# A selective scan on one core: pairs of channel blocks taken in turn, and the sums over states run in quarters of the array

## The chip, the cores and the metric

The kernel runs on one core of one Trainium2 chip. The metric is device time in microseconds (us) of one launch. Before the change three runs took 21455.4, 21479.64 and 21486.99 us; their median is 21479.64 us. One further execution was recorded by the hardware profiler; all views shown here are of that one.

## The reference, cut to what matters

Four layers follow each other on eight images of 56 x 56 tokens with 192 channels: a Toeplitz gate, windowed attention, a depthwise convolution, and a state space layer (a selective scan in four directions). The change lies in the last. Its core, per image, direction and channel (384 channels, 16 states, 3136 tokens):

```python
delta = jax.nn.softplus(delta + delta_bias[None, :, :, None])
dA = jnp.exp(delta[:, :, :, None, :] * A[None, :, :, :, None])
dBu = (delta * u)[:, :, :, None, :] * Bm[:, :, None, :, :]
# hs[t] = dA[t] * hs[t - 1] + dBu[t], for each channel and state
y = jnp.einsum('bkdnl,bknl->bkdl', hs, Cm)     # the sum over the 16 states
return y + Dp[None, :, :, None] * u
```

The four directions' y are added; a normalization over the 384 channels with gain `ln_g` and bias `ln_b`, a product with silu(z) and a projection `out_proj_w` to 192 channels follow, and the result is added to the layer's input.

## The kernel before, in words

All data are fp32. A tensor is laid out with channels on the 128 partitions, so the 384 channels are three blocks d = 0, 1, 2, and tokens lie along the free dimension. The tokens of an image are cut into seven chunks of 448. Directions are called slots; they run in the order 2, 3, 0, 1.

**Stages.** Up to about 3423 us the kernel makes the convolution kernels of the Toeplitz layer, that layer's products for all images, and the whole preparation (`front`, L944: `gate`, `attention`, `conv2`, `inner`, `steps`) of image 0. From there to the end the scan runs: 8 images x 4 directions x 7 chunks = 224 chunks. The front of image b + 1 runs beside the scan of image b, and `finish` (L951) runs for each chunk of the last direction, beside the scan as well.

**The scan.** A chunk holds 24 pairs, numbered g over the whole scan (list `pairs`, L1018): three channel blocks d, and for each of them k = 0..7, where a pair stands for two states (NG = 2). In the order before, all eight k of one d follow each other. For one pair:

- `inject` (L1059, GpSimd): du times B into a slot of `ring` (six slots).
- `decay` (L1076, ScalarE): two exponentials into a bank pair `ps_a` of PSUM (two of them).
- `scan` (L1085, VectorE): the recurrence. It writes over the ring slot if `on_pool(d, k)` holds and over the PSUM tile otherwise.
- `times_c` (L1091): times C into `hc`, of which there are four buffers. It runs on GpSimd where `on_pool` holds (even k) and on VectorE otherwise.
- `keep_state` (L1098) and `initial` (L1066), ScalarE: two columns each.
- `add_up` (L1106, TensorE): for each of the two states a matmul of `ident` (128 x 128) with `hc`, which adds hc to a bank `ps_y` in PSUM. There are two such banks; one holds the sum of one block d over all 16 states.
- `sums` (L1116 in slot 2, else L1118, VectorE): adds the bank to `ysum` in SBUF once all eight k are in; in slot 2 it also adds D times x, for which the x tile is loaded again (`load_xc`, L1032).

An fp32 matmul appears in the trace as two MATMUL records, each with its LDWEIGHTS record, so L1106 has four of each per pair.

**What sets the order.** Scheduling is written out by hand. The loop over g (from L1259) emits for each step: the injection for g + 2 (`feed`), the GpSimd product of pair g - 1, the decay of g + 1, the scan of g, the VectorE product of g if it is one, perhaps a `sums`, then `parts.step`, which emits pieces of `front` and `finish` where a planner (`Parts`, L1121) with rough costs per engine thinks that they fit, and last `add_up(g - 2)`. Each engine's queue is in order, so whatever `parts.step` put on TensorE stands ahead of that `add_up`. The planner emits at most one bank of a client's matmuls in a step: a generator yields `(held, needs)` and stops while it holds a bank. The two banks `ps_f` are for these pieces. The planner counts `add_up` as 1.1 us of TensorE per pair, through `summed[g - 2] = run("E", 1.1, ...)`.

`sums(i, d - 1)` is emitted at k = 4 of the next block, three steps after the last `add_up` of its bank; its x tile is asked for at k = 2. B and C for the next chunk are loaded (`load_bc`, L1027) one k at a time during d = 2. DMAs of the scan and of the front share the SP queue; `inner` stores silu(z) with one DMA per block at L888.

## Time and profile before

| what | value |
|---|---|
| median of three runs | 21479.64 us |
| the profiled execution's own time | 21510.71 us |
| its span, first to last instruction | 21508.5 us |
| first and last scan instruction | 3423 and 21472 us |
| TensorE busy | 17461.0 us (81%) |
| VectorE busy | 15779.7 us (73%) |
| GpSimd busy | 15095.0 us (70%) |
| ScalarE busy | 12490.5 us (58%) |
| mean granted TensorE clock | 0.865 |

How to read it: busy shares are means over stages with different limits, so the stretches of one image's scan have to be taken apart. Names in the profile: PE is TensorE, PEld its weight loads, DVE is VectorE, ACT is ScalarE, POOL is GpSimd, SP is the queue that issues most DMAs. A busy PE is not a PE at its peak, since the end of a matmul includes time in which the next one already runs; the distance between two starts tells how many fit. A group's line shows "busy us, mean ns of one | idle of its engine just before it, and what ended that idle time".

### The profile page before, as it was taken

To read this page: it belongs to the slowest core of one execution; us is meant where nothing else is said; L and a number is where in the kernel's file an instruction comes from. 1 tells how busy PE (TensorE), PEld (TensorE's weight loads), DVE (VectorE), ACT (ScalarE), POOL (GpSimd) and SP (SyncE) were. 2 spreads that over 40 slices of the span, in tenths; PEclk is the share of its full clock that TensorE was granted. 3 is DMA by queue.
4 is the path that set the end of the run, shared out by engine and by line. 5 is a ranking of instruction groups with operands and counts; after the bars stand their busy time and mean duration, and the time that the engine had idled before them with its cause. 6 is when DMAs were issued, how large, how long until landed. Compare 5 with 4: busy or idle time off the path is not lost. (4 is left out here: it accounts for less than half of the span.)

```text
span 21508.5 us, 203992 instructions
## 1 busy us (share of the span) xinstructions
PE 17461.0 (81%) x59404; PEld 9086.2 (42%) x59404; DVE 15779.7 (73%) x12469; ACT 12490.5 (58%) x31833; POOL 15095.0 (70%) x9176
## 2 busy tenths in 40 slices
PE   7878678887887789877987788879877888787777
PEld 4845455433443344433543354334433443333333
DVE  2122116996799668977898779867987789789998
ACT  3126113666666566757575657666666667575555
POOL 0000005887788678867897778878887788689999
PEclk9587757998998889888998899889988999888888
DMA  3931676456544755466545654565446554754444
GB/s 88 248 97 39 190 211 181 131 159 213 172 142 134 217 166 152 134 183 199 160 128 172 209 157 138 159 212 170 140 148 214 173 146 132 218 180 147 134 131 128
DMA packets 2566532, 3470.45 MB, mean 161 GB/s; under 512 B 936270, under 2 KB 2518704, under 8 KB 2534578
## 3 DMA queue, kind: packets, MB, share of 16 engines
q1 hardware_dynamic: 2542724, 3340.61, 52.4%
q0 software_dynamic: 15520, 116.14, 1.5%
q8 instruction: 473, 7.75, 0.2%
q14 instruction: 647, 5.30, 0.1%
q10 hardware_dynamic: 7168, 0.65, 0.0%
HBM read 2822.68 MB, written 634.11 MB: 161 GB/s over the span
## 5 line engine op out<-in xcount | busy, mean ns | idle before, releaser
L1106 PE MATMUL ps_y<-hc,ident_sb 128*128 128x448 f32 x21504 | 10003.9, 603 | 828.4 <-POOL hc L1091 750.6
L1059 POOL TENSOR_TENSOR ring<-du,bm 128x896 f32<-128x896 f32 x5376 | 9450.8, 1775 | 745.8 <-ACT ring L1066 383.2
L1076 ACT ACTIVATE ps_a<-delta,A_logs_sb 128x449 f32<-128x449 f32 x10752 | 6859.6, 638 | 354.3 <-DVE ring L1085 97.7
L1106 PEld LDWEIGHTS ps_y<-hc,ident_sb 128*128 128x128 f32 x21504 | 4315.8, 210 | 5154.2 <-issue 3636.4
L1091 POOL TENSOR_TENSOR hc<-ring,cm 128x896 f32<-128x896 f32 x2688 | 4769.2, 1774 | 1930.7 <-DVE ring L1085 922.1
L1085 DVE TENSOR_TENSOR_SCAN ps_a<-ps_a,ring 128x898 f32<-128x898 f32 x2688 | 5428.3, 2019 | 607.8 <-ACT ps_a L1076 558.2
L1085 DVE TENSOR_TENSOR_SCAN ring<-ps_a,ring 128x898 f32<-128x898 f32 x2688 | 5424.1, 2018 | 571.8 <-ACT ps_a L1076 407.1
L1091 DVE TENSOR_TENSOR hc<-ps_a,cm 128x896 f32<-128x896 f32 x2688 | 2935.2, 1092 | 1037.6 <-PE ps_y L1106 808.0
L1098 ACT COPY state<-ps_a 128x2 f32<-128x2 f32 x2687 | 426.5, 159 | 2783.3 <-DVE hc L1091 2775.4
L287 DVE COPY tzx<-ps_tz 112x448 f32<-112x448 f32 x432 | 269.9, 625 | 1442.5 <-PE ps_tz L281 1292.4
L281 PE MATMUL ps_tz<-tzx,tm 112*112 112x112 f32 x4608 | 1031.1, 406 | 344.7 <-DMA tm<-ext 295.9
L295 POOL DMA_DIRECT2D o<-tzx x192 | 97.3, 513 | 1579.6 <-DVE tzx L287 1341.0
L281 PEld LDWEIGHTS ps_tz<-tzx,tm 112*112 112x112 f32 x4608 | 1021.8, 319 | 385.7 <-issue 381.9
L1066 ACT COPY ring<-state 128x2 f32<-128x2 f32 x4608 | 823.0, 179 | 532.2 <-POOL hc L1091 531.1
L666 PE MATMUL ps_f<-ident_sb,slab 98*98 98x98 f32 x1344 | 336.5, 325 | 602.9 <-ACT slab L659 602.7
L1098 ACT COPY state<-ring 128x2 f32<-128x2 f32 x2688 | 504.1, 188 | 489.6 <-DVE ring L1085 476.2
L1042 POOL TENSOR_TENSOR du<-delta,xcd 128x448 f32<-128x448 f32 x672 | 659.8, 982 | 20.0 <-DMA slab<-in_w_p_dram 19.6
L83 PE MATMUL ps_f<-slab 96*32 96x448 f32 (+7 forms) x2432 | 588.4, 548 | 75.9 <-DMA slab<-pad 55.9
L234 PE MATMUL ps_qv<-wqv,xn 96*128 96x384 f32 (+1 forms) x1200 | 530.3, 525 | 135.6 <-ACT sl L236 68.0
L666 PEld LDWEIGHTS ps_f<-ident_sb,slab 98*98 98x98 f32 x1344 | 202.5, 157 | 1017.5 <-ACT slab L659 798.5
L503 PE MATMUL ps_f<-ident_sb,slab 112*96 112x112 f32 x4704 | 534.7, 268 | 99.7 <-DVE slab L511 49.8
L503 PEld LDWEIGHTS ps_f<-ident_sb,slab 112*96 112x96 f32 x4704 | 513.1, 170 | 239.0 <-issue 121.6
(221 smaller groups left out, 16398.9 us busy)
## 6 DMA issues: line engine op xcount, KB each, us to landing
bm<-bc SPq DMA_DIRECT2D x1792, 448.0 KB
cm<-bc SPq DMA_DIRECT2D x1792, 448.0 KB
xcd<-xc SPq DMA_DIRECT2D x840, 224.0 KB
dl<-slab SPq DMA_DIRECT2D x224, 672.0 KB
delta<-dl SPq DMA_DIRECT2D x224, 672.0 KB
slab<-pad SPq DMA_DIRECT2D x504, 232.0 KB
tzx<-qv SPq DMA_DIRECT2D x192, 588.0 KB
o<-tzx POOLq DMA_DIRECT2D x192, 588.0 KB, 14.2
```

Of the source, the lines that this page charges most:

```text
L83: return f(*args, **kw)
L281: nc.tensor.matmul(po[:, c, :], t[:, :, c2 + c], x[:, :, c1 + c2 + c], start=True, stop=True)
L503: nc.tensor.matmul(p[:CP, t * TT : (t + 1) * TT], ot[:, n % 2, i, t, c % 2 * CP : c % 2 * CP + CP], ident[:TT, :TT], start=i == 0, stop=i ...
L666: nc.tensor.transpose(p[:PT_, e * PT_ : (e + 1) * PT_], S[:, 3 * g + e, :], ident[:PT_, :PT_])
L1042: nc.gpsimd.tensor_mul(du[:, 0, :], deltas[i][:, d, 1 : CH + 1], xcs.pop((i, d)))
L1059: nc.gpsimd.tensor_mul(hs[:, :, tokens(i)[0]], dus[i, d].to_broadcast([128, NG, CH]), bms[i, k])
L1066: nc.scalar.copy(in_ring(g)[:, :, tokens(i)[1]], src)
L1076: nc.scalar.activation(dA[:, n, :], deltas[i][:, d, at : at + CH + 1], AF.Exp, scale=negA[:, slot, d, c : c + 1])
L1085: nc.vector.tensor_tensor_scan(h, dA, hs, 0.0, ALU.mult, ALU.add)
L1091: (nc.gpsimd if on_pool(d, k) else nc.vector).tensor_mul(hc, h[:, :, tokens(i)[0]], cms[i, k])
L1098: nc.scalar.copy(states[i][:, d, NG * k : NG * k + NG], h[:, :, tokens(i)[2]])
L1106: nc.tensor.matmul(yps[i, d][:, :CH], ident, hcs[g][:, n, :], start=k + n == 0, stop=k + n == NP + NG - 2)
```

## The change

1. **Order of pairs.** For each chunk the blocks d = 0 and d = 1 take turns: (0, k = 0), (1, k = 0), (0, k = 1), and so on for 16 steps; d = 2 follows with its eight. `on_pool` becomes "d = 0, or d = 2 and k even", so even steps of a chunk still multiply by C on GpSimd and odd ones on VectorE.
2. **`add_up` runs every second step, for two pairs.** For d = 2 it makes the same four matmul calls for two pairs as before. For a pair of d = 0 and d = 1 with the same k it makes, for each state n, four calls of 64 x 64: `ident[rows, rows]` with half the partitions of one hc. Rows 0-63 of both blocks go to bank u = 0 (block 0's to partitions 0-63, block 1's to 64-127), rows 64-127 of both to bank u = 1 (block 0's to 64-127, block 1's to 0-63). So two banks are open at once, and each holds halves of both blocks.
3. **What follows from mixed banks.** `ysum[:, 0]` and `ysum[:, 1]` hold mixed channels; D, `ln_g`, `ln_b` and `w_out` are permuted on the host (`mixed`), silu(z) is stored mixed (two DMAs of 64 partitions in place of one for d < 2), and the x tile of slot 2 is loaded by `load_mixed` (two DMAs in place of one).
4. **When things are emitted.** With `at` the step in the chunk: `sums` for banks 0 and 1 at 17 and 18, for bank 2 at step 1 of the next chunk; the x tiles of slot 2 at 12, 15 and 21; a wait for `ending` at 16 in place of 12. Other loads stay at their steps.
5. **The planner's books.** `run("E", ...)` is called once per two pairs: 1.1 for d < 2, 2.2 for d = 2.

The core of the diff:

```diff
-        pairs = [(i, d, k) for i in range(len(chunks)) for d in range(ND) for k in range(NP)]
+        pairs = [
+            (i, d, k) for i in range(len(chunks)) for ds in ((0, 1), (2,)) for k in range(NP) for d in ds
+        ]
...
-            return k % 2 == 0
+            return d == 0 or d == 2 and k % 2 == 0
...
             if k == 0:
-                yps[i, d] = psy.tile([128, 512], F32, name="ps_y")
+                for u in (0, 1) if d == 0 else (2,):
+                    yps[i, u] = psy.tile([128, 512], F32, name="ps_y")
+            if d == 2:
+                for q in range(2):
+                    for n in range(NG):
+                        nc.tensor.matmul(
+                            yps[i, 2][:, :CH],
+                            ident,
+                            hcs[g + q][:, n, :],
+                            start=k + q + n == 0,
+                            stop=k + q + n == NP + NG - 2,
+                        )
+                return
+            lo, hi = slice(0, 64), slice(64, 128)
             for n in range(NG):
-                nc.tensor.matmul(
-                    yps[i, d][:, :CH], ident, hcs[g][:, n, :], start=k + n == 0, stop=k + n == NP + NG - 2
-                )
+                for u, at, q, rows in ((0, lo, 0, lo), (0, hi, 1, lo), (1, hi, 0, hi), (1, lo, 1, hi)):
+                    nc.tensor.matmul(
+                        yps[i, u][at, :CH],
+                        ident[rows, rows],
+                        hcs[g + q][rows, n, :],
+                        start=k + n == 0,
+                        stop=k + n == NP + NG - 2,
+                    )
...
-                done = (i, d - 1) if d else (i - 1, ND - 1)
-                if k == 2 and g > NP and chunks[done[0]][1] == 2:
-                    xds[done] = load_xc(*done)
+                if slot == 2 and at in (12, 15, 21):
+                    u = (12, 15, 21).index(at)
+                    xds[i, u] = load_mixed(i, u)
...
-                if k == 4 and g > NP:
-                    sums(*done)
+                if at in (17, 18):
+                    sums(i, at - 17)
+                if i and at == 1:
+                    sums(i - 1, 2)
...
-                if g >= 2:
+                if g and g % 2 == 0:
                     add_up(g - 2)
-                    summed[g - 2] = run("E", 1.1, taken[g - 2])
+                    summed[g - 2] = summed[g - 1] = run("E", 1.1 if d < 2 else 2.2, taken[g - 2], taken[g - 1])
```

and in `inner`, and the new loader:

```diff
-                    nc.sync.dma_start(out=dst[:, d, :], in_=src)
+                    if dst is z_d[b] and d < 2:
+                        for h in range(2):
+                            to = (h ^ d) * 64
+                            nc.sync.dma_start(out=dst[to : to + 64, h, :], in_=src[64 * h : 64 * h + 64])
+                    else:
+                        nc.sync.dma_start(out=dst[:, d, :], in_=src)
...
+        def load_mixed(i, u):
+            b, slot, j = chunks[i]
+            t = sp.tile([128, CH], F32, name="xcd", bufs=3)
+            for h in range(2):
+                half, d = (slice(64 * u, 64 * u + 64), u ^ h) if u < 2 else (slice(64 * h, 64 * h + 64), 2)
+                src = xc_d[slot // 2][b][half, d, j * CH : (j + 1) * CH]
+                nc.sync.dma_start(out=t[64 * h : 64 * h + 64], in_=src)
+            return t
```

More of the change, by code (lines that the diff above doesn't have):

```diff
@@ L1103, in add_up, with sums @@
             if k == 0:
-                yps[i, d] = psy.tile([128, 512], F32, name="ps_y")
-            for n in range(NG):
-                nc.tensor.matmul(
-                    yps[i, d][:, :CH], ident, hcs[g][:, n, :], start=k + n == 0, stop=k + n == NP + NG - 2
-                )
-        def sums(i, d):
+                for u in (0, 1) if d == 0 else (2,):
[12 more added lines that the diff above has]
+            lo, hi = slice(0, 64), slice(64, 128)
+            for n in range(NG):
+                for u, at, q, rows in ((0, lo, 0, lo), (0, hi, 1, lo), (1, hi, 0, hi), (1, lo, 1, hi)):
[6 more added lines that the diff above has]
+                    )
+        def sums(i, u):
             b, slot, j = chunks[i]
-            y = yps[i, d][:, :CH].rearrange("p (u v) -> p u v", v=H)
-            yv = scan_view(ysum[:, d], slot, j)
+            y = yps[i, u][:, :CH].rearrange("p (u v) -> p u v", v=H)
+            yv = scan_view(ysum[:, u], slot, j)
             if slot == 2:
-                x = xds.pop((i, d)).rearrange("p (u v) -> p u v", v=H)
-                nc.vector.scalar_tensor_tensor(yv, x, Dsum[:, d : d + 1], y, ALU.mult, ALU.add)
+                x = xds.pop((i, u)).rearrange("p (u v) -> p u v", v=H)
+                nc.vector.scalar_tensor_tensor(yv, x, Dsum[:, u : u + 1], y, ALU.mult, ALU.add)
             else:
@@ L1261, in model @@
                     b_next += 1
-                more = i + 1 < len(chunks)
-                if more and d == 1 and k == 0:
+                more, at = i + 1 < len(chunks), g % (ND * NP)
+                if more and at == 8:
                     b1, slot1, j1 = chunks[i + 1]
@@ L1269, in model @@
                         xcs[i + 1, e] = load_xc(i + 1, e)
-                if more and (d, k) == (2, 0):
+                if more and at == 16:
                     xcs[i + 1, 2] = load_xc(i + 1, 2)
-                if more and (d, k) in ((1, 6), (1, 7), (2, 6)):
-                    times_x(i + 1, k - 6 if d == 1 else 2)
+                if more and at in (14, 15, 22):
+                    times_x(i + 1, min(at - 14, 2))
                     run("P", 0.93)
@@ L1293, in model @@
                     load_bc(pi + 1, pk)
-                done = (i, d - 1) if d else (i - 1, ND - 1)
-                if k == 2 and g > NP and chunks[done[0]][1] == 2:
-                    xds[done] = load_xc(*done)
-                if i % (4 * NCH) == 0 and b > 0 and (d, k) == (1, 4):
+                if slot == 2 and at in (12, 15, 21):
+                    u = (12, 15, 21).index(at)
+                    xds[i, u] = load_mixed(i, u)
+                if i % (4 * NCH) == 0 and b > 0 and at == 16:
                     while ending.at < 3:
                         parts.step(anything, ending)
-                if k == 4 and g > NP:
-                    sums(*done)
+                if at in (17, 18):
+                    sums(i, at - 17)
+                if i and at == 1:
+                    sums(i - 1, 2)
                 pb, pslot, pj = chunks[i - 1]
-                if i and pslot == 1 and (d, k) == (0, 5):
+                if i and pslot == 1 and at == 5:
                     while ending in parts.clients:
@@ L1310, in model @@
                 parts.step({"A": max(n2, fed[g + 2]) - 0.7, "E": n1 + 5.0, "D": 0.2})
-                if g >= 2:
+                if g and g % 2 == 0:
                     add_up(g - 2)
-                    summed[g - 2] = run("E", 1.1, taken[g - 2])
-            if on_pool(d, k):
-                times_c(last)
-            for g in (last - 1, last):
-                add_up(g)
+                    summed[g - 2] = summed[g - 1] = run("E", 1.1 if d < 2 else 2.2, taken[g - 2], taken[g - 1])
+            add_up(last - 1)
             while parts.clients:
                 parts.step(anything)
-            sums(i, d)
+            sums(i, 2)
             drain(finish(b, j))
@@ L1356, in parts, with mixed @@
         return v.reshape((-1, p) + v.shape[1:]).swapaxes(0, 1)
+    def mixed(v):
+        w = v.copy()
+        w[64:, 0], w[:64, 1], w[64:, 1] = v[:64, 1], v[64:, 1], v[64:, 0]
+        return w
     def with_bias(w, b):
@@ L1401, in layouts @@
     a["A_logs"] = np.asarray(i[p + "A_logs"]).reshape(4, ND, 128, NS)[order].transpose(2, 0, 1, 3)
-    a["Ds"] = np.asarray(i[p + "Ds"]).reshape(4, ND, 128).transpose(2, 1, 0)
-    a["ln_g"], a["ln_b"] = parts(i[p + "ln_g"], 128), parts(i[p + "ln_b"], 128)
-    a["w_out"] = parts(np.asarray(i[p + "out_proj_w"]).T, 128)
+    a["Ds"] = mixed(np.asarray(i[p + "Ds"]).reshape(4, ND, 128).transpose(2, 1, 0))
+    a["ln_g"], a["ln_b"] = mixed(parts(i[p + "ln_g"], 128)), mixed(parts(i[p + "ln_b"], 128))
+    a["w_out"] = mixed(parts(np.asarray(i[p + "out_proj_w"]).T, 128))
     a.update(constants())
```

## The prediction

> **What bounds the kernel now.** I read the page first, then the stretches of one image's scan, then the waits, and last the order of time inside two stretches. From the page, the busy row of TensorE and the groups that the change touches or that stand behind it (busy us, mean ns, idle time before it and what ended it):

> ```profile
> PE 17461.0 (81%) x59404; PEld 9086.2 (42%) x59404; DVE 15779.7 (73%) x12469; ACT 12490.5 (58%) x31833; POOL 15095.0 (70%) x9176
> L1106 PE MATMUL ps_y<-hc,ident_sb 128*128 128x448 f32 x21504 | 10003.9, 603 | 828.4 <-POOL hc L1091 750.6
> L1091 DVE TENSOR_TENSOR hc<-ps_a,cm 128x896 f32<-128x896 f32 x2688 | 2935.2, 1092 | 1037.6 <-PE ps_y L1106 808.0
> ```

> The adds over states are the largest TensorE group, and VectorE's products stand still 808 us for them: an hc buffer is free only after its add. The mean hides the stages, so here are the scan of image 3 cut by direction (beside it run gate and attention; attention; conv2 and inner; steps, finish and the next gate), and 14 chunks of the last image, beside which no front runs. Columns: length, then PE, PEld, DVE, ACT, POOL busy, clock, DMA.

> ```profile
> 10430.00:10973.00 543.00, 476.47 (x1764) 253.78 (x1763) 487.98 (x390) 353.83 (x984) 462.16 (x277) 0.93 0.52 151
> 10973.00:11481.00 508.00, 419.11 (x1517) 206.69 (x1516) 481.59 (x402) 372.72 (x1176) 459.38 (x275) 0.92 0.41 127
> 11481.00:12134.00 653.00, 492.65 (x1671) 206.49 (x1670) 470.02 (x337) 364.36 (x827) 457.96 (x273) 0.86 0.69 207
> 12134.00:12770.00 636.00, 546.45 (x1743) 285.18 (x1742) 473.78 (x335) 421.48 (x900) 490.65 (x298) 0.91 0.57 170
> 20078.00:20984.00 906.00, 663.10 (x1339) 285.66 (x1339) 869.99 (x547) 506.74 (x1344) 905.72 (x544) 0.87 0.41 133
> ```

> The last row is a floor: without a front, POOL is full (906 of 906), 64.7 us a chunk. With one, a chunk takes 73 to 93 us and no engine is full; what is missing are waits between engines. Inside `inner` the order of time shows one limit clearly:

> ```profile
> 11811.84 1.67 PE L840 MATMUL ps_f<-slab 96*128 96x448 f32 x4
> 11813.34 1.67 PE L1106 MATMUL ps_y<-hc,ident_sb 128*128 128x448 f32 x4
> 11814.85 1.67 PE L840 MATMUL ps_f<-slab 96*128 96x448 f32 x4
> 11815.05 1.09 DVE L1091 TENSOR_TENSOR hc<-ps_a,cm 128x896 f32<-128x896 f32 x1 [0.37 <-PE ps_y L1106]
> 11816.35 1.67 PE L1106 MATMUL ps_y<-hc,ident_sb 128*128 128x448 f32 x4
> 11817.86 1.67 PE L840 MATMUL ps_f<-slab 96*128 96x448 f32 x4
> ```

> Four records start every 1.505 us, 0.376 us each, without a gap: two pairs take 6.02 us, while DVE needs 2 x 2.02 + 1.09 = 5.13 and POOL 3 x 1.775 = 5.32. Here PE is the bound. Whether small tiles run side by side is seen here (L869: 32 columns wide; L928: 12 rows, two row groups, two banks):

> ```profile
> 12018.60 2.46 PE L869 MATMUL ps_f<-slab 96*32 96x448 f32 x24
> 12020.99 3.27 PE L1106 MATMUL ps_y<-hc,ident_sb 128*128 128x448 f32 x8
> 12024.20 2.09 PE L869 MATMUL ps_f<-slab 96*32 96x448 f32 x20
> 12089.78 1.02 PE L928 MATMUL ps_f<-slab,w_dt_sb 12*128 12x448 f32 x4
> 12090.74 1.77 PE L1106 MATMUL ps_y<-hc,ident_sb 128*128 128x448 f32 x4
> ```

> 24 records of L869 occupy 2.39 us, where one after the other would be 24 x 0.376 = 9.0: four columns at a time, 6 x 0.376 = 2.26, and the rest is a switch. Four of L928 take 0.96 in place of 1.50: two rows at a time, 0.75, and two switches. L869 and L1106 together repeat every 5.60 us (12018.60 to 12024.20) against 2.26 + 3.01 = 5.27, so two switches cost 0.33.

> [...] The trace agrees for columns and for rows separately; both at once it doesn't show. [...] during the scan 3806 of 18049 us have half clock, and records of L1106 then start 0.75 apart.

> **The change part by part.** Durations are of the profiled execution, 21510.7 us (span 21508.5 and 2.2 around it).

> *Quarters.* Two pairs cost 8 x 0.376 = 3.01 us of PE. As quarters they are 16 records in 4 rounds of four, 1.50, plus up to two switches[...]: 1.50 to 1.83. Saved: 1.2 to 1.5, I take 1.3. With 8 such double steps a chunk, 10.4 us of PE a chunk; over 224 chunks 2330 us, but only where PE ends a wait. If only rows or only columns overlapped, the saving is nil and the switches stay (bounds -1.5 and +0.3).

> *What it can give at most.* For the first 16 steps of each chunk I compared the length with the busiest of DVE, POOL and ACT and cut the difference at 10.4: 217, 159, 435 and 410 us in the four directions, 2 in the last nine chunks. Sum 1223 us.

> *What it gives.* DVE idle time during the scan is 3015 us. Sorted by the step in which it falls (0 to 15 are the changed ones) and by what ended it:
> - L1091 on DVE behind L1106: 286 us in waits under 4 us, which are PE's plain backlog (as 0.37 above): gone. 293 us in 43 waits over 4 us, where PE itself stood behind a DMA or another engine (the page has up to 171 us for L869 behind pad loads): the stall stays, its backlog drains faster; a third, 98.
> - scans behind ScalarE (L1076): 657 us in the changed steps. Half of it is Silu and Softplus on large tiles, which stays; some is ScalarE behind a front product that PE gave late (L879 waits 376 us for L869): a fifth, 130.
> - DVE's front instructions behind PE (L791 189, L966 72, L1001 59, L522 58, L511 44, sum 422): a sixth, 70.
> - L1116 behind its x tile, 46 us: the tile is now asked for 3 to 5 steps ahead in place of 2: gone, 46.

> Sum of gains 630 us.

> *What it adds.* `sums` had three steps between the last add and itself; now banks 0 and 2 have one. DVE's queue is in order, so all scans stand behind such a wait, and ScalarE's decay behind those. From the trace I took, for each chunk, the end of the adds as now emitted and the end of the DVE product ahead of the new place. With PE as late as now, bank 0's sum at 17 would wait 198 us in all (132 of 224 chunks), bank 2's at step 1, whose second pair's adds come 1.6 us later than the first's, 446 us (182 of 223). PE will be less late: at 17 eight cheap double steps precede it, I take 40 us; at step 1 the four dear double steps of d = 2 do, I take 1.0 us in each of the 189 chunks before the last 35: 190. In the last 35, POOL is the bound and hides it. Sum 230; both ends, 0 and 644, are kept.

> *At nothing.* DVE, POOL and ACT do the same instructions at the same steps (even steps multiply on POOL, as before). Bank 0 of the next chunk waits for the sum at step 1, but so it does for that step's product. `load_mixed` adds 168 issues to SP, the store of z 16, at 0.33 to 0.47 us each: about 80 us on a queue that nobody but these tiles waits for by the trace; the tiles at 15 and 16 wait for the du product of step 14 or 15, with B and C loads behind them, which are needed five or more steps later. B and C of k > 0 are now needed later than before, so POOL's 60 us behind L1027 can only shrink. The planner sees less TensorE work, so it may place front pieces sooner; it is mostly held to one bank a step, so I leave the density as it is.

> Net: 21510.7 - 630 + 230 = 21111. The profiled execution is 31 us above the median, so against the median: **21080 us**, 1.9% less.

> **The rivals.**
> - *Likeliest (0.50)*: as worked out, own range 20850 to 21300. PE's backlog goes, DVE and POOL bound gate and attention, the rest remains DMA and ScalarE waits.
> - *The whole room (0.25)*: with PE early, ScalarE gets its products early, and the chains of steps 2 and 3 (653 and 636 us against 470 to 490 of DVE) close too. For it: no engine is full there. Against: waits over 4 us end in DMAs. Three quarters of 1223: 21480 - 920 = 20560.
> - *Slower: the sums wait in place of the products (0.13).* [...] at half clock a quarter round takes 0.75, a double step 3.0 as now, PE stays as late as it is, and DVE waits 644 us at `sums`. Only the x tiles' 46 and a third of the 630 come back (210): 21480 + 644 - 210 = 21910. It decides from 630 / 224 = 2.8 us of waits per chunk at the sums. Against: where the front is dense, PE keeps 1.7 + 3.0 busy of 5.3.
> - *The quarters don't overlap (0.03)*: with two at a time the price is that of before and switches come on top, 0.3 x 1792 = 540 at most, about 21700; with none it is 3 us on each of 1792 double steps and far above.
> - *Hidden anyway (0.09)*: DMA and ScalarE waits take over all that PE gives back, 21480.

> **How the numbers follow.** A measurement of this kernel can tell about 0.2% from no change. Faster: 0.50 + 0.25 and a little of the last, 0.76. Same: 0.09. Slower: 0.15, the two cases with more than 21520. Below 20500 I leave a third of the second case (0.08). Above 21560 I leave most of the two slower ones (0.12): their waits grow from nothing to the full 644, so a few of their times fall short of it. The range of 8 in 10 is 20500 to 21560.

> **What would show it.** Records of L1106's successor with 64*64, 16 in about 1.5 to 1.8 us at full clock; if 3 us, the overlap failed. DVE's wait before hc behind PE from 808 to below 350 us. A new wait of DVE before `ysum`, about 230 us; over 630 and the slower rival is right. The last chunks at 64 to 67 us as before. The first direction's stretch from 543 to about 515 us, the third's from 653 to about 620. The mean granted clock lower than 0.865. The prediction is wrong if the third and fourth stretches fall to under 560 us, or if the clock falls so far that a double step costs 3 us.

## The result and the profile after

The changed kernel is slower: median 21653.57 us (21646.47 to 21661.52, 4 runs) against 21467.52 us for the kernel before beside it; ratio 1.0086, 95% interval 1.0069 to 1.0104. The profiled execution took 21661.52 us, 150.8 us more than that of before, and its scan 18203 us, 154 more.

TensorE's row of the page and the groups that answer to those shown of before:

```profile
PE 16039.7 (74%) x73740; PEld 7669.1 (35%) x73740; DVE 15806.1 (73%) x12469; ACT 12488.4 (58%) x31833; POOL 15099.6 (70%) x9176
L1139 PE MATMUL ps_y<-hc,ident_sb 64*64 64x448 f32 x28672 | 4350.6, 712 | 817.9 <-POOL hc L1108 708.2
L1128 PE MATMUL ps_y<-hc,ident_sb 128*128 128x448 f32 x7168 | 3399.4, 625 | 355.1 <-POOL hc L1108 272.3
L1108 DVE TENSOR_TENSOR hc<-ps_a,cm 128x896 f32<-128x896 f32 x2688 | 2934.7, 1092 | 356.7 <-PE ps_y L1139 94.1
```

The quarters do what they should. The adds held TensorE for 10004 us and now hold it for 4351 + 3399 = 7750 (busy time as the page counts it: at full clock a record lasts 0.54 us there, and the next starts 0.376 us after it). VectorE's products (L1108, before L1091), which stood 820 us behind the adds, now stand 165 us. (Both are summed over the whole trace; the page's 808 leaves out waits of under 0.15 us.) The gain is given back at `sums`, further on in VectorE's queue. The main group of `sums` before, then the two groups now, from the lists of groups by form:

```profile
L1118 DVE TENSOR_TENSOR ysum<-ysum,ps_y 128x448 f32<-128x448 f32 x504 | 366.6, 727 | 2.2 <-PE ps_y L1106 2.2
...
L1155 DVE TENSOR_TENSOR ysum<-ysum,ps_y 128x448 f32<-128x448 f32 x504 | 374.2, 742 | 669.9 <-PE ps_y L1128 435.4 <-PE ps_y L1139 233.7
L1153 DVE SCALAR_TENSOR_TENSOR ysum<-xcd,Dsum,ps_y 128x448 f32<-128x448 f32 x168 | 177.7, 1057 | 161.5 <-PE ps_y L1128 95.7 <-PE ps_y L1139 59.8 <-DMA slab<-x 2.5
```

435 + 234 + 96 + 60 = 825 us of VectorE's time pass before `ysum`, all behind the adds of its bank; before the change it was 2. By step, 531 us fall at step 1 (bank 2, 179 waits) and 294 at step 17 (bank 0, 146 waits). While VectorE stands there, TensorE works at adds for 631 us and at the front's matmuls for 160. On average over these waits, the bank's last batch starts only 0.6 us (bank 0) and 0.9 us (bank 2) before VectorE arrives, though its products have been ready for 4.2 and 4.9 us. One of them in order of time, in the attention stretch, VectorE and TensorE alone:

```profile
11005.23 2.01 DVE L1102 TENSOR_TENSOR_SCAN ps_a<-ps_a,ring 128x898 f32<-128x898 f32 x1
...
11006.51 0.92 PE L1128 MATMUL ps_y<-hc,ident_sb 128*128 128x448 f32 x2
11007.26 2.80 PE L596 MATMUL ps_f<-slab 96*96 96x392 f32 x8
11007.46 1.09 DVE L1108 TENSOR_TENSOR hc<-ps_a,cm 128x896 f32<-128x896 f32 x1 [0.22 <-PE ps_y L1128]
...
11009.90 3.17 PE L1128 MATMUL ps_y<-hc,ident_sb 128*128 128x448 f32 x8
...
11013.10 1.05 DVE L1153 SCALAR_TENSOR_TENSOR ysum<-xcd,Dsum,ps_y 128x448 f32<-128x448 f32 x1 [4.55 <-PE ps_y L1128]
11013.98 2.00 DVE L1102 TENSOR_TENSOR_SCAN ring<-ps_a,ring 128x898 f32<-128x898 f32 x1
```

VectorE ends its product at 11008.55 and next in its queue is the sum. (The queue keeps the emitted order: between one sum and the next the trace has 1, 7 and 16 scans in turn, through waits of up to 13.1 us.) The two pairs' adds (eight records) start at 11009.90, because two front groups (eight records of L596, four to a step) stood ahead of the batch. They end at 11013.07, and VectorE has lost 4.55 us, with the next scan behind the sum. Before, one group stood ahead of each pair's adds, as in the same work of the kernel before:

```profile
11101.42 1.48 PE L596 MATMUL ps_f<-slab 96*96 96x392 f32 x4
11102.74 1.67 PE L1106 MATMUL ps_y<-hc,ident_sb 128*128 128x448 f32 x4
11104.25 1.48 PE L596 MATMUL ps_f<-slab 96*96 96x392 f32 x4
11105.57 1.67 PE L1106 MATMUL ps_y<-hc,ident_sb 128*128 128x448 f32 x4
```

While a front runs beside the scan, the front work directly ahead of one emission of adds had a median of 1.14 us before and has 2.49 us (quarters) and 2.39 us (whole matmuls) now, and the whole batch is as long as the adds of two pairs.

The stretches of image 3 again, cut by direction at the changed kernel's own times, and 14 chunks of the last image:

```profile
10453.20:11003.30 550.10, 428.16 (x2190) 206.68 (x2189) 494.58 (x399) 353.43 (x1007) 463.55 (x277) 0.85 0.51 146
11003.30:11543.10 539.80, 394.31 (x1929) 170.34 (x1928) 484.39 (x403) 365.75 (x1150) 459.68 (x275) 0.78 0.41 124
11543.10:12192.70 649.60, 455.09 (x2150) 164.08 (x2149) 464.49 (x327) 380.30 (x847) 458.57 (x273) 0.80 0.70 212
12192.70:12823.40 630.70, 513.24 (x2304) 253.33 (x2303) 478.13 (x346) 413.12 (x890) 488.83 (x298) 0.86 0.57 168
20219.00:21129.60 910.60, 545.01 (x2239) 189.39 (x2239) 865.35 (x547) 512.17 (x1344) 910.14 (x546) 0.76 0.41 135
```

PE is less busy everywhere, and no stretch with a front is clearly shorter: 550, 540, 650 and 631 us after 543, 508, 653 and 636. Attention's is 32 us longer. Summed over the seven images that have a front beside them, the four directions took 3772, 3709, 4423 and 4278 us and now take 3821, 3931, 4359 and 4221: attention's loses 222 us, more than the third and fourth gain. The last image is POOL's, as it was.

### The profile page after: what moved, and what is told of

It reads as the page before. It is cut to its first block, busy times and chain, and to the rows that moved or that the text cites. A ratio compares the mean times of both kernels' runs of the same rounds, so it can differ in the third digit from the quotient of the medians.

```text
span 21659.7 us, 232733 instructions
## 1 busy us (share of the span) xinstructions
PE 16039.7 (74%) x73740; PEld 7669.1 (35%) x73740; DVE 15806.1 (73%) x12469; ACT 12488.4 (58%) x31833; POOL 15099.6 (70%) x9176
## 5 line engine op out<-in xcount | busy, mean ns | idle before, releaser
L1076 POOL TENSOR_TENSOR ring<-du,bm 128x896 f32<-128x896 f32 x5376 | 9463.9, 1779 | 602.7 <-ACT ring L1083 351.4
L1108 POOL TENSOR_TENSOR hc<-ring,cm 128x896 f32<-128x896 f32 x2688 | 4781.2, 1779 | 2241.6 <-issue 543.0
L1139 PE MATMUL ps_y<-hc,ident_sb 64*64 64x448 f32 x28672 | 4350.6, 712 | 817.9 <-POOL hc L1108 708.2
L1128 PE MATMUL ps_y<-hc,ident_sb 128*128 128x448 f32 x7168 | 3399.4, 625 | 355.1 <-POOL hc L1108 272.3
L1108 DVE TENSOR_TENSOR hc<-ps_a,cm 128x896 f32<-128x896 f32 x2688 | 2934.7, 1092 | 356.7 <-PE ps_y L1139 94.1
L1139 PEld LDWEIGHTS ps_y<-hc,ident_sb 64*64 64x64 f32 x28672 | 1197.4, 165 | 3237.6 <-issue 1685.1
L1128 PEld LDWEIGHTS ps_y<-hc,ident_sb 128*128 128x128 f32 x7168 | 1538.2, 222 | 2053.4 <-issue 1462.0
L1155 DVE TENSOR_TENSOR ysum<-ysum,ps_y 128x448 f32<-128x448 f32 x504 | 374.2, 742 | 669.9 <-PE ps_y L1128 435.4
L933 PE MATMUL ps_f<-slab,w_dt_sb 12*128 12x448 f32 x1176 | 444.0, 727 | 434.7 <-ACT slab L925 276.4
```

Of the source, the lines that this page charges most:

```text
L933: nc.tensor.matmul(held[s][:, :CH], w_dt[row, o, d * 128 : (d + 1) * 128], rc[row, n % 2, :], start=True, stop=True)
L1076: nc.gpsimd.tensor_mul(hs[:, :, tokens(i)[0]], dus[i, d].to_broadcast([128, NG, CH]), bms[i, k])
L1108: (nc.gpsimd if on_pool(d, k) else nc.vector).tensor_mul(hc, h[:, :, tokens(i)[0]], cms[i, k])
L1128: nc.tensor.matmul(yps[i, 2][:, :CH], ident, hcs[g + q][:, n, :], start=k + q + n == 0, stop=k + q + n == NP + NG - 2,)
L1139: nc.tensor.matmul(yps[i, u][at, :CH], ident[rows, rows], hcs[g + q][rows, n, :], start=k + n == 0, stop=k + n == NP + NG - 2,)
```

## The experiments

Three theories at the start. A: `sums`, one step behind their adds, wait in place of the products. B: TensorE, less busy, spends 6684 us of the scan at half clock (3800 before), and the front's short chains are slower. C: the planner, told of half the adds, places front pieces worse. D came later: TensorE arrives early at an add and holds up the front's matmuls behind it. Times are medians, ratios those to the kernel before beside them. That kernel took 21467 to 21492 us in the different rounds, so runs of different rounds are compared by their distances from the kernel before beside them (the change: 186 us slower); by the intervals, such a comparison is good to some 40 us.

**a1: sums that wait for nobody, read from SBUF.**

```diff
-            y = yps[i, u][:, :CH].rearrange("p (u v) -> p u v", v=H)
+            y = deltas[i][:, u, 1 : CH + 1].rearrange("p (u v) -> p u v", v=H)
```

> The changed kernel, with one edit: each sums instruction on VectorE adds a tile that has long been in SBUF (the chunk's delta) in place of the bank in PSUM, so the scan's result is left out of the output and VectorE never waits for TensorE there; all else stays. Theory A (the sums, one step behind their last adds, have taken the place of the waits that the quarters removed): the 825 us that VectorE stands before ysum go, some of it comes back before hc or behind ScalarE; 20850 to 21100 us. Theory B (TensorE, less busy, runs 6686 us at half clock in place of 3806, and the front's short chains, attention's above all, are slower for it): only what lies at the sums and not in the chains comes back, 21450 to 21600 us. Theory C (the planner, told of half the adds, puts front pieces in worse places): 21400 to 21600 us.

21651.8 us, 1.0071 (1.0051 to 1.0091): no theory's number. The edit was bad: the mean L1155 went from 742 to 1499 ns. Its control says the same.

**a2: the same edit in the kernel before.**

> The kernel before with the same edit as a control: sums adds the chunk's delta in place of the bank, so the scan's result is left out of the output. VectorE waited 2 us before ysum behind TensorE and 47 us behind the x tile, which is still loaded. All theories: the same as before, 21400 to 21480 us. If it were some hundred us faster, the reading of the bank itself, not the wait, would cost, and the run on the changed kernel would say less.

21755.08 us, 1.0117 (1.0099 to 1.0134). With both inputs in SBUF the instruction took 1224 ns in place of 727 (the last section says when). a1 and a2 settle nothing on the wait; b1 and d4 repeat them with an input in PSUM.

**a3: order, batches, sums and books of the change, whole matmuls.** The channels stay unmixed, so loads and stores are those of before.

```diff
-            for n in range(NG):
-                for u, at, q, rows in ((0, lo, 0, lo), (0, hi, 1, lo), (1, hi, 0, hi), (1, lo, 1, hi)):
+            for q in range(2):
+                for n in range(NG):
                     nc.tensor.matmul(
-                        yps[i, u][at, :CH],
-                        ident[rows, rows],
-                        hcs[g + q][rows, n, :],
+                        yps[i, q][:, :CH],
+                        ident,
+                        hcs[g + q][:, n, :],
...
```

> The changed order of pairs, adds for two pairs every second step and the sums at steps 17, 18 and 1, but no quarters: blocks 0 and 1 each go to their own bank with whole 128 x 128 matmuls, channels are not mixed. TensorE then has the work of before. Theory A: TensorE is as late as before and the sums stand right behind it, and products before hc wait as well: clearly slower than the changed kernel, 21800 to 22200 us, with over 825 us before ysum. Theory B: the clock is that of before (0.86) and the short chains are fast again: faster than the changed kernel, 21400 to 21600 us. Theory C: the planner's books are those of the changed kernel, so about 21650 us.

22091.32 us, 1.0275 (1.0258 to 1.0292), at a clock of 0.856. VectorE stands 802 us before `ysum` and 209 before hc. A's forecast came true and B's did not: with nearly the old clock it is slower still. It also splits the change in two: everything but the quarters costs 22091 - 21491 = 600 us, and the quarters give 600 - 186 = 414 us.

**a4: late sums.**

```diff
-                if at in (17, 18):
-                    sums(i, at - 17)
-                if i and at == 1:
+                if at in (18, 20):
+                    sums(i, (at - 18) // 2)
+                if i and at == 2:
                     sums(i - 1, 2)
```

> The changed kernel with the sums later, as far as two banks allow without moving an add: bank 0 at step 18 in place of 17, bank 1 at 20 in place of 18, bank 2 at step 2 in place of 1. A scan of 2.02 us lies between the old and the new place of banks 0 and 2. Theory A: of 825 us before ysum some 400 go, and TensorE waits 0.7 us more often for a bank: 21250 to 21450 us, faster than before for the first time. Theory B and C: nothing of weight, 21600 to 21660 us.

21409.87 us, 0.996 (0.9947 to 0.9972): 81 us faster than before, so 267 us are won back, as A forecast. VectorE's waits before `ysum` fall from 825 to 208 us. Its own view of waits, with what took their place:

```profile
DVE ring L1102 <- ACT ps_a L1093: 633.5, 322, 9.3
DVE ps_a L1102 <- ACT ps_a L1093: 621.7, 324, 9.2
...
DVE ysum L1155 <- PE ps_y L1128: 161.3, 66, 13.5
```

617 us of waits gone are 267 us of time: scans behind ScalarE's decay rise from 997 to 1255 us, and TensorE now waits 235 us for a bank (63 in the change).

**b1: sums that wait for nobody, read from PSUM.**

```diff
-            y = yps[i, u][:, :CH].rearrange("p (u v) -> p u v", v=H)
+            y = das[g][:, 0, :CH].rearrange("p (u v) -> p u v", v=H)
```

> The changed kernel; each sums adds the current pair's tile in PSUM (ps_a, just written by VectorE itself) in place of the bank ps_y, so the scan's result is left out of the output, VectorE waits for nobody there, and one input still comes from PSUM, as in the changed kernel. (Reading a second SBUF tile, tried before, made the instruction itself 0.5 to 0.75 us longer and hid the answer.) ScalarE's decay of two pairs on waits for that read, 0.7 us. Theory A: the 825 us before ysum go and part returns behind ScalarE: 20950 to 21250 us. Theories B and C: 21450 to 21600 us.

21371.12 us, 0.9959 (0.9945 to 0.9973), between the two forecasts and 97 us faster than before. The wait is gone entirely and 283 us come back, not 400 to 700. From its view of waits:

```profile
DVE ps_a L1102 <- ACT ps_a L1093: 733.2, 335, 10.3
DVE ring L1102 <- ACT ps_a L1093: 656.5, 326, 9.8
```

1390 us behind ScalarE, where the change has 997 and the kernel before had 965: VectorE, freed of TensorE, meets ScalarE. a4 and b1 are faster than the kernel before at clocks of 0.80, so the lower clock alone did not turn the sign.

**d4: b1's control, the same edit in the kernel before.**

> The control for the sums that wait for nobody: the kernel before, each sums adding the current pair's PSUM tile in place of its bank, so the scan's result is left out of the output. VectorE waited 2 us there. Within 40 us of 21470; what it differs by is what the edit itself costs in the run on the changed kernel, where ScalarE's decay waits for that read too.

21506.3 us, 1.0007 (1.0000 to 1.0014). The edit itself costs some 15 us, so b1's 283 us is the price of the wait to within about that.

**b2: TensorE kept busy.** On a4, zeros are added to the open banks at seven odd steps of each chunk.

```diff
+                if at % 2 and 3 <= at < 16:
+                    keep_busy(i)
```

`keep_busy` makes eight 64 x 64 calls of `ident[rows, none]`, a quarter of the identity that holds only zeros, with the chunk's delta.

> The kernel with the late sums (18, 20, 2; 21410 us), and at the odd steps 3 to 15 of each chunk TensorE also adds zero eight times (64 x 64 quarters of the identity that hold only zeros, times delta), 1.5 us of work at full clock that waits for nothing and whose result nobody waits for beyond the bank's own sum. Theory B (the clock): half-clock time falls from 6607 us towards 4000, the front's chains are fast again, attention's direction above all: faster, 21200 to 21350 us. Otherwise TensorE's lost time shows: 21450 to 21600 us.

21925.89 us, 1.0217 (1.0202 to 1.0232). The clock came back to 0.86 (half clock for 4127 us in place of 6607), and the kernel was 458 us slower than before, 539 slower than a4; attention's direction, summed over the seven images, rose from 3765 to 3881 us. The waits before `ysum` were 226 us, much as a4's 208. B's gain did not come. What half clock alone costs stays open, since the work that restores it costs more.

**b3: the books of before, with late sums.**

```diff
-                    summed[g - 2] = summed[g - 1] = run("E", 1.1 if d < 2 else 2.2, taken[g - 2], taken[g - 1])
+                    summed[g - 2] = summed[g - 1] = run("E", 2.2, taken[g - 2], taken[g - 1])
```

> The kernel with the late sums (21410 us), and the planner told 2.2 us of TensorE for every two pairs, as before the change; the matmuls stay quarters. Theory C (front pieces are placed worse): 21200 to 21350 us. Otherwise within 40 us of 21410.

21287.18 us, 0.9917 (0.9902 to 0.9932), 181 us less than before and some 100 better than a4: C holds too, though these books count the quarters as dearer than they are.

**b4: batches one step later**, with the sums at 19, 21 and 3.

```diff
-                if g and g % 2 == 0:
-                    add_up(g - 2)
+                if g > 2 and g % 2:
+                    add_up(g - 3)
```

> The changed kernel with each batch of adds one step later (at odd steps, for the pairs three and two steps back) and the sums at 19, 21 and 3, so that the distance between adds and sums is that of the late sums or more. Theory D (TensorE's queue is in order, it now arrives early and stands before an add for GpSimd's product, 981 us, with the front's matmuls behind it): the product is ready when the add comes up, front products are earlier, 21150 to 21350 us. Otherwise as the late sums, 21380 to 21450 us, or slower if products before hc now wait for their buffer.

21507.09 us, 1.0021 (1.0013 to 1.0028), some 120 us slower than a4. Almost no wait is left before `ysum` (2 us), but VectorE's products before hc stand 964 us behind the adds, more than the 820 of before, and GpSimd's 1925: the four hc buffers are freed a step too late. D's forecast failed; what D's wait alone costs this run can't tell, since the buffers now set the pace.

**c1: only the books of before, in the changed kernel** (b3's line, sums at 17, 18 and 1).

> The changed kernel with one edit: the planner counts 2.2 us of TensorE for every two pairs, as before the change, in place of 1.1 for blocks 0 and 1; sums at 17, 18 and 1. Theory C (the lighter books put front pieces in worse places, 123 us with the late sums): 21500 to 21560 us, the waits before ysum smaller too, since fewer front matmuls stand ahead of a batch of adds. If the books cost only with the late sums: 21620 to 21660 us.

21590.13 us, 1.0055 (1.0040 to 1.0070), 118 us more than before: some 70 us better than the change, hardly beyond the spread, and between the two forecasts. Waits before `ysum` are 639 us.

**c2: light books in the kernel before** (0.55 us for a pair of blocks 0 and 1).

> The kernel before with one edit: the planner counts 0.55 us of TensorE for a pair of blocks 0 and 1 in place of 1.1; every matmul stays. Theory C: the books alone cost here too, and more, since the matmuls are not cheaper: 21550 to 21800 us. Otherwise within 40 us of 21470.

21509.11 us, 1.0017 (1.0008 to 1.0025): some 37 us, within the 40 that were expected if the books do not matter here. By this run and c1, the change's books cost some 40 to 70 us of its 186.

**c3: late sums and dear books** (b3's line with 3.0).

> The kernel with the late sums and the planner told 3.0 us of TensorE for every two pairs, more than both before (2.2) and true for quarters (1.7). Theory C in its simple form (the books hold front pieces back, and the less is crowded ahead of a batch the better): at or below 21287 us, the time with 2.2. If the front is held back too far, its end moves past the scan of the image before it and the scan waits for it: above 21350 us.

21166.94 us, 0.9856 (0.9842 to 0.9871): faster than both kernels, 305 us below the one before and 491 better than the change.

**c4: b1 and b3 together.**

> Sums that wait for nobody (they add the pair's own PSUM tile, so the scan's result is left out of the output) together with the books of before (2.2 for two pairs): both costs that the change brought are gone and the quarters stay. If the two costs add up: 21371 - 120 = 21250 us or less; below 21000 us would be the room that the prediction saw (630 us of gains, 20850). If it stays at 21200 or above, the rest of the predicted gain is lost elsewhere: VectorE's waits behind ScalarE (967 us before) would then be well above 1100 us.

21317.74 us, 0.9928 (0.9912 to 0.9945). The two gains do not clearly add: 154 us less than before, 57 beyond b1. Scans stand some 1280 us behind ScalarE. The prediction's 630 us aren't there even where the sums cost nothing.

**d1: dear books in the kernel before** (1.5 us a pair).

> The kernel before with one edit: the planner counts 1.5 us of TensorE for each pair (3.0 for two) in place of 1.1. If the planner's crowding was a cost of the kernel all along, and the change only inherited and sharpened it: 21150 to 21300 us, and the 242 us that dear books gave the late sums belong to the books alone. If it hurts only together with batches of adds and one step to the sums: within 60 us of 21470.

21364.09 us, 0.9943 (0.9928 to 0.9958), 128 us less than the kernel before and between the forecasts: more than half of what dear books give the late sums (305 - 81 = 224 us) was to be had before the change. On equal books the quarters with late sums win by 305 - 128 = 177 us.

**d2: dear books only, in the changed kernel.**

> The changed kernel, sums at 17, 18 and 1 as it has them, with the planner told 3.0 us for every two pairs. Late sums gave 244 us with the change's books and 303 with 2.2. If the two causes are independent: 21654 - 240 = 21410 us. If sparser front pieces alone bring TensorE early enough for the sums: below 21300 us, with under 400 us before ysum.

21465.02 us, 0.9988 (0.9981 to 0.9995), 27 us less than before and 213 better than the change, with 729 us still before `ysum`. So the books work for the most part not through the sums; they and the late sums are two causes. Together they give 491 us (c3), about 213 + 267.

**d3: dearer books** (3.8), with late sums.

> Late sums and 3.8 us of TensorE in the planner's books for every two pairs. If holding back goes on helping: below 21150 us. If the front is then held back past the scan of the image before it: above 21250 us.

22372.27 us, 1.0412 (1.0394 to 1.0429). The front is held back too long: of image 3's directions the first two take about as long as before (550 and 513 us) and the third is far shorter (491), but the fourth takes 912, where the scan stands still for 207 and once more for 124 us until the next image's data are made. Of the four values tried with late sums (1.1 for blocks 0 and 1, 2.2, 3.0, 3.8) 3.0 is the best.

## Why the prediction was wrong, point by point

- **The quarters: right.** At full clock, what follows sixteen quarter records starts 1.67 us after the first of them (1.50 to 1.83 forecast). From first to last start they take 1.20 us, at half clock 2.3 us. Alone they are worth 414 us (a3 to the change). That all four run together was the author's estimate: the trace of before showed tiles side by side by columns (24 records of L869 in 2.39 us) and by rows (four of L928 in 0.96), each apart; this one shows both at once.
- **Gains, 630 us: right in kind, off in where.** The products' waits shrank by 655 us where 384 was forecast; the x tile's 46 us went, and VectorE's front instructions wait 63 us less for TensorE (70 forecast). But "ScalarE behind a front product that PE gave late: a fifth, 130" went the other way: 965 us behind ScalarE became 997, and 1390 with the sums freed (b1). The old trace held little of this kind: within those 965 us ScalarE itself stood behind a TensorE product for 1 us, and worked at decays and front pieces for most of the rest. An idle time that ends at one engine was counted as gained; the next engine took a good part of it.
- **"What it adds" is the step that failed.** "At 17 ... I take 40 us; at step 1 ... 1.0 us in each of the 189 chunks: 190. Sum 230; both ends, 0 and 644, are kept." Measured: 294 and 531, together 825 us, above even the upper end. The upper end was taken from the lateness of the adds in the old trace, in which one front group stands ahead of each pair's adds. In the new order the pieces of two steps stand ahead of each batch of two pairs, as the lines at 11007.26 and 11009.90 show. That PE would be early after eight cheap double steps was argued from its load, and those 40 us became 294. Cheap adds took nothing off this wait: a3 has 802 us of it with whole matmuls. There, bank 0's last four whole records come first in their batch and take as long as the sixteen quarters (4 x 0.376 us); bank 2's adds are whole in both. b1 prices the wait at 283 us of time and a4 wins back 267, either enough to turn the sign (186). No run undoes the batches alone, so how much of the wait is theirs, and how much comes from the sums' standing one step behind the adds in place of three, is not told apart; a4 shows that one step more takes away three quarters of it.
- **The rival that ends slower had the mechanism.** It expected 644 us at the sums, 2.8 us a chunk as the point from which it decides, and 21910 us; there are 825 us, 3.7 a chunk, and 21654. Its reason, half clock (6684 us of the scan after 3800), is not needed: a3 has 802 us of these waits at nearly the clock of before (0.856). Within the change, 430 of the 825 us lie behind batches that ran at full clock; for 195 of them everything since their products were ready did. How much the half clock adds stays open, since b2 restored the clock only where the sums were late already. Its price left only a third of the gains; the products' waits alone shrank by 655 us, more than the whole of the gains that the forecast counted.
- **"I leave the density as it is" was wrong by some 40 to 70 us.** Told of less work, the planner crowds front pieces (c1, c2), and the kernel would have liked the opposite (c3, d1).
- **At nothing: POOL.** Its products wait 695 us behind the adds in place of 497, probably since a batch frees two buffers at once (argued, not tested); the forecast had nothing there.
- **The marks named in advance.** hc below 350 us, the records, the clock below 0.865 (it was 0.80) and the last image came as said; the first and third stretches (515 and 620 forecast) came at 550 and 650. The mark "over 630 us before `ysum` and the slower rival is right" held. Of the two signs of being wrong neither came: the third and fourth stretches stayed above 560 us, and fewer than 600 of the 1792 double steps ran wholly at half clock.

What stays open: why scans wait more for ScalarE once TensorE is early. That they do is shown. In these waits of b1, ScalarE works at decays for 656 us (454 before), at front pieces for 417 (349), and stands still before a front piece, for a product or a load, for 163 (51); so front pieces are part of it and no more than that, and no run takes them away.

## What to carry to other kernels

When a faster step frees an engine, look for the next instruction in each in-order queue that waits for the same result, and count what stands ahead of the producer in its own queue in the new order, not in the old trace. Batching a producer also batches what waits ahead of it, and the batch's own length counts too; both take slack from its consumer. Here too few steps between add and sum cost about two thirds (267 to 283 of 414 us) of what the faster adds gave. A planner's cost for a step is a knob as much as a truth; after a change of cost, try values on both sides of it.
